# Edge messages of a graph network: more tiles fetched row by row on the SyncE queue, and the receivers of four groups by one DMA

## The chip, the cores and the metric

The kernel runs on one core of one Trainium2 chip. The metric is the device time of one execution in microseconds (us). Before the change it is 4115.59 us, the median of three runs (4114.87 to 4116.8).

## The reference, cut to what matters

One layer of message passing over 12,500 nodes (64 numbers each) and 412,500 edges (32 numbers each), the edges sorted by their receiver. In float32:

```python
h = jnp.maximum(_layernorm(x, axis=-1), 0.0)
msg_in = jnp.concatenate([h[senders], h[receivers], edge_features], axis=-1)
messages = act(msg_in @ W1 + b1) @ W2 + b2          # act is swish
att_logits = act(msg_in @ Wa1 + ba1) @ Wa2 + ba2
att = jax.nn.softmax(att_logits, axis=0)             # over all edges
aggregated = jax.ops.segment_sum(messages * att, receivers, num_segments=N)
upd_in = jnp.concatenate([h, aggregated], axis=-1)
x = x + act(upd_in @ Wu1 + bu1) @ Wu2 + bu2
```

## The kernel before, in words

**Node stage.** The normalized nodes are multiplied once by the sender's and once by the receiver's part of both first-layer weights. The results are two tables in DRAM, `ts_d` (senders) and `tr_d` (receivers), with 128 float32 numbers per node: a row of 512 bytes.

**Edge stage** (`one_pass`). 128 edges make a tile, K = 8 tiles a group, and there are 403 groups. `load(g)` is called two groups ahead of use (AHEAD = 2). For one group it

- issues, on GpSimd (POOL), one indirect DMA for each tile (L487), which fetches the 128 sender rows of the tile into `gs`, a tile with eight buffers;
- for every fourth group (NQ = 4), issues on SyncE (SP) the edge features of four groups, `eo` (L496: partitions 64 to 127, 8192 bytes each), and the receivers' numbers of the same four groups, `db` (L499: two DMAs, for partitions 0 to 31 and 32 to 63; each repeats one row of 8192 bytes of `dst_row` in its 32 partitions), and loads four window positions into registers (L474). `eo` and `db` have two buffers;
- issues on SP two DMAs for a window of receiver rows, `wins` (L506; three buffers);
- calls `rows(q, g)`, which fetches a part of one tile row by row (next paragraph);
- compares `db` with the window's node numbers on VectorE (DVE, L513), which writes the one-hot half of `eo`, and multiplies it on TensorE (PE, L517) with the window: receiver and edge part of eight tiles in the PSUM tile `pe`.

**Rows.** The last tile of some groups is not gathered by POOL. `QUEUES = [(ENG.SP, 11, 0, 12)]` says: on SP, one tile for every 11 groups, starting from group 0, with 12 rows issued in each group. `numbers` (L433) loads the 128 sender numbers of that tile (L438), half a period ahead. In each group, `rows` (L440) loads the next 12 numbers into SP's registers (L460) and issues 12 DMAs of one row, 512 bytes each (L464), into `one_gs` (two buffers). After 11 groups the tile is complete; that group then issues seven gathers in place of eight (L486), and adds the extra tile by an instruction of its own (L525).

**Then** `begin(g)` adds `pe` and `gs` on DVE (L523) and applies tanh on ScalarE (ACT, L526). `end(g)` forms messages and logits on DVE (L536 to L547). `by_node` (L588, L594) and `put` (L618 to L624) sum messages by receiver with a running maximum for the softmax. Between the groups, small parts of the update stage are prepared.

**Order.** Every engine works off its own list in program order; the order on PE, ACT and DVE is that of the calls. On SP the list of a group is: (every fourth group) `eo`, `db`, registers; `wins`, `wins`; register load; the rows. Completion of SP's DMAs is counted in eight counters, which the built program gives out in turn. A DMA first waits until the previous user of its counter, the eighth DMA before it on SP, has landed. The `wins` DMAs also wait for PE to have read that buffer three groups before.

**Update stage.** After the last group, 13 blocks of nodes are finished and written.

The change touches `QUEUES` and the `db` DMAs in `load`.

Of the kernel before, what the change touches and what calls it, by code (L numbers as in the profile page):

```python
# [49 lines left out]
ENG = mybir.EngineType  # L50
# [11 lines left out]
R = 32  # L62
# [4 lines left out]
E2 = H * P  # L67
# [2 lines left out]
NC = 8  # L70
TABLES = 4

QUEUES = [(ENG.SP, 11, 0, 12)]
EPS = 1e-5
NEG = -3.0e38
BIG = 3.0e38
# [288 lines left out]
def one_pass(tc, n_edges, v):  # L365
    nc = tc.nc
# [4 lines left out]
    ts_d, tr_d, bq_d, xb_d, edge, dst_row = (  # L371
        v[k] for k in ("ts_d", "tr_d", "bq_d", "xb_d", "edge", "dst_row"))
# [10 lines left out]
    with ExitStack() as ctx:  # L383
# [30 lines left out]
        with tc.tile_pool(name="work2", bufs=2) as work2, \  # L414
# [25 lines left out]
            def rows(q, g):  # L440
                engine, every, phase, n_rows = QUEUES[q]
                if g == 0:
                    numbers(q, phase + every)
                if g < phase:
                    return
                at = (g - phase) % every
                g = g - at + every
                if at == 0:
                    rows_at.pop((q, g - every), None)
                    if (q, g) in rows_at:  # L450
                        alone[g] = work2.tile([P, C], F32, name=f"one_gs{q}")
                if at == every // 2:
                    numbers(q, g + every)
                if (q, g) not in rows_at:
                    return
                a = at * n_rows
                n = min(n_rows, P - a)
                if n <= 0:
                    return
                load, regs = nc.values_load_multi_w_load_instructions(  # L460
                    rows_at[q, g][0:1, a:a + n], engines=[engine], min_val=0, max_val=NP - 1,
                    skip_runtime_bounds_check_because=WHY)
                for k in range(n):
                    dma[engine].dma_start(alone[g][a + k:a + k + 1, :], ts_d[bass.ds(regs[k], 1), :])  # L464
# [5 lines left out]
                           ap=[[C, NP + WR - SHIFT], [SHIFT * C, 2], [1, C]])  # L470

            def registers(g, engine, at, base=base_sb, top=NP - 1):
                n = min(NQ, NG - g)
                _, regs = nc.values_load_multi_w_load_instructions(  # L474
                    base[0:1, g:g + n], engines=[engine], min_val=0, max_val=top,
                    skip_runtime_bounds_check_because=WHY)
                for i in range(n):
                    at[g + i] = regs[i]

            def load(g):  # L480

                t = g * K
                if g % NQ == 0:
                    registers(g, ENG.SP, at_sp)
                gs = gss[g] = gather.tile([P, K, C], F32, name="gs")
                for j in range(K - (g in alone)):  # L486
                    nc.gpsimd.indirect_dma_start(  # L487
                        out=gs[:, j, :], out_offset=None, in_=ts_d[:, :],
                        in_offset=bass.IndirectOffsetOnAxis(ap=src_sb[:, t + j:t + j + 1], axis=0))
                if g % NQ == 0:  # L490
                    n = min(NQ, NG - g) * E2
                    eo = work2.tile([P, NQ, E2], F32, name="eo")
                    db = work2.tile([WR, NQ, E2], I32, name="db")
                    for i in range(g, min(g + NQ, NG)):
                        ees[i] = eo[:, i - g, :], db[:, i - g, :]
                    nc.sync.dma_start(eo.rearrange("p g e -> p (g e)")[WR:, :n],  # L496
                                      edge[:, g * E2:g * E2 + n])
                    for r in range(2):
                        nc.sync.dma_start(  # L499
                            db.rearrange("p g e -> p (g e)")[r * R:(r + 1) * R, :n],  # L500
                            bass.AP(tensor=dst_row.tensor, offset=dst_row[r:r + 1, g * E2:].offset,
                                    ap=[[0, R], [1, n]]))
                eo, db = ees.pop(g)
                win = wins[g % WINS]
                for r in range(2):
                    nc.sync.dma_start(win[r * R:(r + 1) * R, :, r, :],  # L506
                                      tr_w[bass.ds(at_sp[g], R), :, :])
                for q in range(len(QUEUES)):
                    if QUEUES[q][0] == ENG.SP:
                        rows(q, g)  # L510
                for h in range(2):
                    e = slice(h * E2 // 2, (h + 1) * E2 // 2)
                    pin(nc.vector.tensor_scalar(eo[:WR, e], db[:, e], bj[:, g, h:h + 1], None,  # L513
                                                op0=ALU.is_equal))
                pe = pes[g] = pre_ps.tile([P, K, C], F32, name="pe")
                for q in range(H):
                    pin(nc.tensor.matmul(pe[:, 2 * q:2 * q + 2, :], eo[:, q * P:(q + 1) * P],  # L517
                                         win[:, q // 2, :, :], start=True, stop=True))
# [138 lines left out]
            for g in range(AHEAD):  # L657
                load(g)
            done = 0
            for g in range(NG):  # L660
# [16 lines left out]
                if g + AHEAD < NG:  # L677
                    load(g + AHEAD)
# [358 lines left out]
```

## Time and profile before

| | us |
|---|---|
| median of three runs | 4115.59 |
| the profiled execution | 4115.52 |
| its span, first to last instruction | 4113.8 |
| mean granted TensorE clock | 0.633 |
| first gather starts on POOL | 50.42 |
| first `wins` DMA issued on SP | 86.44 |
| last gather starts on POOL | 4042.24 |
| sum of DVE's waits for `db` at L513 | 151.5 |
| sum of DVE's waits for gathers at L523 | 740.0 |

DMAs by line, of the page's last part: 4608 rows (`one_gs`) of 0.5 KB; 806 windows of 32 KB; 100 `eo` of 512 KB and one of 384; 200 `db` of 256 KB and two of 192; 36 loads of row numbers. The DMA engines are busy 17.0% of the time with SP's queue and 20.8% with POOL's.

A row of a costliest group gives line, engine, operation, what is written and read, how often, the busy time and the mean of one, and then the idle time of the engine before it with what ended it. "Issue" means that the engine waited for nothing the profile shows. SP's and ACT's issuing of DMAs is not counted as busy; it is read from their order of time, where a row names start, duration and, if several equal instructions follow each other, their number. Rows of waits give the total in us, the number of waits and the longest.

### The profile page before, as it was taken

What the parts mean: (1) busy time and instruction counts of PE and PEld (TensorE: products, weight loads), DVE (VectorE), ACT (ScalarE), POOL (GpSimd) and SP (SyncE); (2) the same over time, 40 slices, a digit from 0 to 9 for tenths busy, and PEclk for the clock granted to TensorE, in tenths of its full rate; (3) what the DMA queues carried; (4) which work ended last, traced back from release to release, by engine and by line L of the source; (5) the groups of instructions that cost most, each with busy time, mean ns of one, the idle gap of its engine ahead of it and who ended that gap; (6) DMA issues with size and microseconds to landing.
All of it is one profiled execution on the core that took longest, in us unless ns stands there. A gap on an engine that the chain in (4) does not pass through costs nothing.

```text
span 4113.8 us, 59789 instructions
## 1 busy us (share of the span) xinstructions
PE 2284.8 (56%) x10980; PEld 1852.9 (45%) x10980; DVE 3021.4 (73%) x8518; ACT 584.3 (14%) x1235; POOL 3035.8 (74%) x3213
## 2 busy tenths in 40 slices
PE   5555545555556555556555555555555555555555
PEld 4444434444445444444444444444444444444444
DVE  6777867777777777777777777777777777777777
ACT  3211111111111111111111111111111111111112
POOL 3777777777777777777777777777777777777773
PEclk8666666666565666665566666666666556566665
DMA  7344443443434333333333333333333333333334
GB/s 270 88 102 101 99 105 92 105 101 97 102 93 99 86 91 84 88 91 81 91 84 89 91 81 91 83 89 91 81 91 82 91 91 81 92 81 90 91 78 112
DMA packets 220602, 393.50 MB, mean 96 GB/s; under 512 B 77077, under 2 KB 146554, under 8 KB 207034
## 3 DMA queue, kind: packets, MB, share of 16 engines
q0 software_dynamic: 102016, 209.13, 20.8%
q1 hardware_dynamic: 116826, 170.81, 17.0%
q10 hardware_dynamic: 1376, 9.67, 0.6%
q14 instruction: 294, 2.41, 0.2%
q8 instruction: 90, 1.47, 0.2%
HBM read 363.58 MB, written 25.72 MB: 95 GB/s over the span
## 4 chain that ended last, share of the span: by engine, by line


## 5 line engine op out<-in xcount | busy, mean ns | idle before, releaser
L487 POOL DMA_INDIRECT gs<-ts_d,src_sb x3188 | 3018.7, 947 | 1022.1 <-issue 952.1
L517 PE MATMUL pe<-wins,eo 128*128 128x256 f32 x3224 | 1477.3, 638 | 967.7 <-DVE eo L513 819.6
L517 PEld LDWEIGHTS pe<-wins,eo 128*128 128x128 f32 x3224 | 1000.5, 325 | 1265.8 <-DVE eo L513 970.2
L523 DVE TENSOR_TENSOR gs<-pe,gs 128x1024 f32<-128x1024 f32 (+1 forms) x403 | 487.7, 1211 | 775.5 <-DMA gs<-ts_d,src_sb 740.0
L526 ACT ACTIVATE pe<-gs 128x1024 f32<-128x1024 f32 x403 | 413.8, 1027 | 2585.7 <-DVE gs L523 1997.7
L588 DVE TENSOR_SCALAR wt<-iota_w,dloc,p 128x40 f32<-128x40 f32 x3224 | 734.0, 320 | 0.1
L594 PE MATMUL sp<-wt,acts 128*65 128x40 f32 x6448 | 608.9, 267 | 0.7 <-DVE wt L588 0.7
L594 PEld LDWEIGHTS sp<-wt,acts 128*65 128x65 f32 x6448 | 578.7, 183 | 1.0 <-DVE wt L588 0.8
L605 PEld LDWEIGHTS mt<-ss,w2u 65*128 65x128 f32 x806 | 224.8, 293 | 371.3 <-issue 321.5
L513 DVE TENSOR_SCALAR eo<-db,bj 64x256 f32<-64x256 int32 x806 | 259.7, 360 | 158.6 <-DMA db<-in_dst_row_dram 151.5
L564 PE MATMUL mt<-ident,mx 128*128 128x128 f32 x103 | 45.1, 437 | 547.3 <-DVE sums L622 538.2
L605 PE MATMUL mt<-ss,w2u 65*128 65x40 f32 x806 | 184.9, 324 | 261.4 <-DVE gm L571 257.9
L542 DVE SCALAR_TENSOR_TENSOR pe<-pe,gs 128x512 f32<-128x512 f32 x403 | 281.3, 698 | 13.0
L544 DVE TENSOR_TENSOR pe<-pe,w_all 128x512 f32<-128x512 f32 x403 | 281.4, 698 | 12.8
L536 DVE SCALAR_TENSOR_TENSOR acts<-pe,gs 128x512 f32<-128x512 f32 x403 | 278.2, 690 | 15.7 <-ACT pe L526 4.0
L547 DVE TENSOR_REDUCE lg<-pe 128x8 f32<-128x512 f32 x403 | 278.4, 691 | 13.7
L564 PEld LDWEIGHTS mt<-ident,mx 128*128 128x128 f32 x103 | 18.4, 179 | 557.7 <-issue 556.0
L624 DVE COPY stand<-nmax 64x40 f32 x806 | 163.4, 203 | 0.6
L622 DVE TENSOR_TENSOR sums<-sums,mt 64x40 f32 x600 | 113.2, 189 | 15.0 <-PE mt L605 10.9
L575 ACT ACTIVATE scale<-fall 128x1 f32<-128x1 f32 x103 | 20.9, 203 | 645.1 <-DVE fall L574 629.2
L600 ACT COPY ss<-sp 65x40 f32<-65x40 f32 x403 | 73.5, 182 | 20.7 <-PE sp L594 20.3
L618 DVE SCALAR_TENSOR_TENSOR sums<-sums,scale,mt 64x40 f32 x206 | 51.6, 251 | 11.4 <-PE mt L605 7.3
(92 smaller groups left out, 577.7 us busy)
## 6 DMA issues: line engine op xcount, KB each, us to landing
one_gs<-ts_d SPq DMA_DIRECT2D x4608, 0.5 KB
eo<-in_edge_dram SPq DMA_DIRECT2D x100, 512.0 KB
db<-in_dst_row_dram SPq DMA_DIRECT2D x200, 256.0 KB
gs<-ts_d,src_sb POOLq DMA_INDIRECT x3188
wins<-tr_d SPq DMA_DIRECT2D x806, 32.0 KB
ts_d<-ts SPq DMA_DIRECT2D x5, 896.0 KB
tr_d<-tr ACTq DMA_DIRECT2D x5, 896.0 KB
hT_d<-hT ACTq DMA_DIRECT2D x1, 3136.0 KB
```

What stands on the lines that cost most here:

```text
L487: nc.gpsimd.indirect_dma_start(out=gs[:, j, :], out_offset=None, in_=ts_d[:, :], in_offset=bass.IndirectOffsetOnAxis(ap=src_sb[:, t + j:t ...
L513: pin(nc.vector.tensor_scalar(eo[:WR, e], db[:, e], bj[:, g, h:h + 1], None, op0=ALU.is_equal))
L517: pin(nc.tensor.matmul(pe[:, 2 * q:2 * q + 2, :], eo[:, q * P:(q + 1) * P], win[:, q // 2, :, :], start=True, stop=True))
L523: pin(nc.vector.tensor_tensor(gss[g][:, :n, :], pes[g][:, :n, :], gss[g][:, :n, :], ALU.add))
L526: pin(nc.scalar.activation(pes[g], gss[g], AF.Tanh))
L536: pin(nc.vector.scalar_tensor_tensor(acts[g % ACTS][:, :, 0:U], th[:, :, U:C], 1.0, gs[:, :, U:C], op0=ALU.add, op1=ALU.mult))
L542: pin(nc.vector.scalar_tensor_tensor(att, th[:, :, 0:U], 1.0, gs[:, :, 0:U], op0=ALU.add, op1=ALU.mult))
L544: pin(nc.vector.tensor_tensor(att, att, wa2[:, None, :].to_broadcast([P, K, U]), ALU.mult))
L547: pin(nc.vector.tensor_reduce(lgs[s][:, k:k + K], att, AX.X, ALU.add))
L588: pin(nc.vector.tensor_scalar(wt[:, j, :], iota_w[:, j // H, :], dloc[:, g * K + j:g * K + j + 1], p[:, k + j:k + j + 1], op0=ALU.is_equal ...
L594: pin(nc.tensor.matmul(sp, acts[g % ACTS][:, j, :], wt[:, j, :], start=j == 0, stop=j == K - 1))
L605: pin(nc.tensor.matmul(pp, w2u.rearrange("s h u -> s (h u)"), sps.pop(g), start=True, stop=True))
```

## The change

Two edits:

- `QUEUES` changes from one tile per 11 groups with 12 rows per group to one tile per 9 groups with 16 rows per group. 16 rows in eight groups make 128; in the ninth group none is issued. 44 tiles (5632 rows) are fetched in this way in place of 36 (4608 rows), and POOL issues 3180 gathers in place of 3188.
- The two `db` DMAs for four groups become one. Its source has three dimensions: 2 rows of `dst_row`, each repeated 32 times, 2048 numbers. Its destination is 64 partitions of 2048 numbers.

```diff
@@ -70,7 +70,7 @@
-QUEUES = [(ENG.SP, 11, 0, 12)]
+QUEUES = [(ENG.SP, 9, 0, 16)]
@@ -495,11 +495,10 @@
                     nc.sync.dma_start(eo.rearrange("p g e -> p (g e)")[WR:, :n],
                                       edge[:, g * E2:g * E2 + n])
-                    for r in range(2):
-                        nc.sync.dma_start(
-                            db.rearrange("p g e -> p (g e)")[r * R:(r + 1) * R, :n],
-                            bass.AP(tensor=dst_row.tensor, offset=dst_row[r:r + 1, g * E2:].offset,
-                                    ap=[[0, R], [1, n]]))
+                    a, b = (dst_row[r:r + 1, g * E2:].offset for r in range(2))
+                    nc.sync.dma_start(
+                        db.rearrange("p g e -> p (g e)")[:2 * R, :n],
+                        bass.AP(tensor=dst_row.tensor, offset=a, ap=[[b - a, 2], [0, R], [1, n]]))
```

From there on, the lines of the changed kernel are one lower than those of before: L513 becomes L512, L506 becomes L505, L523 becomes L522.

## The prediction

> **What bounds the kernel now.** I read the busy shares, the slices, the costliest groups, then POOL's order of time, SP's waits and order of time, and the busy time by window. First the page:
>
> ```profile
> PE 2284.8 (56%) x10980; PEld 1852.9 (45%) x10980; DVE 3021.4 (73%) x8518; ACT 584.3 (14%) x1235; POOL 3035.8 (74%) x3213
> ...
> POOL 3777777777777777777777777777777777777773
> ...
> L487 POOL DMA_INDIRECT gs<-ts_d,src_sb x3188 | 3018.7, 947 | 1022.1 <-issue 952.1
> ```
>
> POOL and DVE look equally busy, but POOL's idle time is nearly all "issue": it waits for nobody. Its order of time shows the pitch:
>
> ```profile
> 4012.28 0.94 POOL L487 DMA_INDIRECT gs<-ts_d,src_sb  x1 [0.30 <-issue]
> 4013.53 0.94 POOL L487 DMA_INDIRECT gs<-ts_d,src_sb  x1 [0.30 <-issue]
> ```
>
> The steady pitch is 1.248 us (26 steps take 32.46 us at the end). The gathers run from 50.42 to 4043.18 us; 3188 x 1.248 = 3979 of these 3993 us. So POOL's list of gathers is the bound: 403 groups, 31.6 gathers per four groups, 39.5 us per four groups. DVE needs 3021/403 = 7.5 us per group, 30 us per four.
>
> The second chain is SyncE's. Its waits, and three stretches of its order of time:
>
> ```profile
> SPq L506 <- PE pe L517: 291.7, 69, 9.9
> SPq L506 <- PE mt L605: 256.1, 138, 10.8
> ...
> SPq L464 <- DMA db<-in_dst_row_dram: 88.9, 118, 1.4
> ```
>
> ```profile
> 96.40 0.87 SPq L506 DMA_DIRECT2D wins<-tr_d  x2
> 98.45 4.83 SPq L464 DMA_DIRECT2D one_gs<-ts_d  x12
> 103.53 0.86 SPq L506 DMA_DIRECT2D wins<-tr_d  x2
> ...
> 2038.26 0.49 SPq L496 DMA_DIRECT2D eo<-in_edge_dram  x1
> 2038.80 1.04 SPq L499 DMA_DIRECT2D db<-in_dst_row_dram  x2
> ...
> 2118.98 0.49 SPq L496 DMA_DIRECT2D eo<-in_edge_dram  x1
> 2119.52 1.04 SPq L499 DMA_DIRECT2D db<-in_dst_row_dram  x2
> 2121.36 0.87 SPq L506 DMA_DIRECT2D wins<-tr_d  x2
> 2123.22 6.05 SPq L464 DMA_DIRECT2D one_gs<-ts_d  x12
> ```
>
> A group's undisturbed SP work is 7.10 us (96.40 to 103.53, the next pair 7.10 later), a row (4.83-0.23)/11 = 0.417 us, the head of four groups (eo to wins) 2.38 us. Per four groups that is about 30.1 us, plus about 0.9 us of waiting for db, of 39.5. SP has 8 us to spare, and spends it waiting for PE. The third row of its waits matters most: a row DMA waits for the **receivers' DMA to land**, because SP's DMAs take eight completion counters in turn and each first waits for the eighth one before it. Today that costs at most 1.4 us.
>
> **The change, part by part.**
>
> *Gathers.* 44 tiles in place of 36 leave POOL: 8 x 1.248 = -10.0 us while POOL is the bound. POOL per four groups: 39.4 us. DVE gets 8 more split additions, 8 x (1089+280-1223 ns) = 1.2 us, hidden in its slack.
>
> *Rows.* 8 of 9 groups issue 16 rows, one none. Four rows more are 4 x 0.417 = 1.67 us. The load of row numbers into registers (L460) takes 0.933 us for 12 values and the one at L474 0.488 for 4, so 16 values should take 1.15, +0.22. A group with rows becomes 7.10+1.67+0.22 = 8.99 us; one without about 1.1 us (two wins DMAs at 0.43 and the 0.25 us gap). Four groups on average: 4 x (8 x 8.99 + 1.1)/9 = 32.4. One db issue fewer saves 0.53 of the head: 1.85. The sum is **34.3 us of SP issue per four groups, against POOL's 39.4**. Alone, this would be hidden, with 5.1 us to spare. Eight more loads of row numbers at 0.25 us vanish in it.
>
> *One DMA for the receivers.* Bytes are the same: 64 rows of 8192 B, 524 kB per four groups. What changes is the shape: the source goes from 32 x 2048 (twice) to 2 x 32 x 2048. [...]
>
> What does it cost? The rows on transfers, by window (after PE, PEld, DVE, ACT, POOL: granted clock, DMA share, GB/s):
>
> ```profile
> 1.00:20.00 19.00, 5.97 (x22) 4.51 (x23) 15.30 (x22) 7.91 (x14) 1.14 (x8) 1.00 0.94 362
> 2039.00:2046.00 7.00, 3.19 (x23) 2.71 (x21) 3.29 (x7) 0.00 (x0) 5.17 (x7) 0.74 0.93 202
> 2056.00:2077.00 21.00, 11.94 (x65) 10.12 (x64) 15.59 (x45) 3.13 (x5) 15.83 (x17) 0.66 0.24 61
> ```
>
> Today eo and db of four groups fill all 16 engines for 7 us. A busy engine moves 362/(16 x 0.94) = 24.1 GB/s in the first window and only 202/(16 x 0.93) = 13.6 in the burst; the gathers alone keep each engine 24% busy.
> - Lower end, two engines at 24.1 GB/s and nothing beside: 262 kB / 24.1 = 10.9 us; with the gathers' 24% beside, 14.3 us.
> - Upper end, by the burst: db's half of it, 3.5 us, is 150 GB/s. [...]
> - [...] I take **19.3 us**, between the ends.
>
> Before db's rows come eo's: half of the burst, over at about 2042.4, 3.6 us after the db issue at 2038.80. So db lands L = 3.6+19.3 = 22.9 us after its issue (today: 7).
>
> *Who waits.* In the built program db is followed by two wins DMAs and five rows; the sixth row takes db's counter and waits. SP reaches it 1.31 (to wins) + 1.86 + 0.22 + 5 x 0.417 = 5.5 us after the db issue. The stall is 22.9-5.5 = 17.4 us. Queued behind it on SP are ten rows of this group (4.2 us) and then the wins DMAs of the next group, for which PE's L517 waits, and behind PE DVE's L523. The wins and rows already issued stand behind db in the queue of those engines too, but land right after it. SP runs three groups ahead at most (three wins buffers), so the lead pays for one such stall, not for one every four groups: the mean rate decides. SP per four groups: 34.3+17.4 = **51.7 us, against 39.5 today**. DVE reaches L513 of the new four groups early and waits there for the same landing.
>
> **The sum.** 396 groups issue rows, 99 times four: 99 x (51.7-39.5) = +1208 us. The gathers' -10 us no longer counts, since POOL now waits for gs buffers. At the start SP's first wins (86.4) is 36 us behind POOL's first gather, a lag that today is caught up and then is not; at the end eight groups go without rows, which gives about that back. Own time of the profiled execution 4115.5 (span 4113.8; the median of the runs, 4115.6, is the same): 4115.5+1208 = about **5320 us**.
>
> **The rivals.**
> 1. *SP stalls on the slow db* (above): ends for the transfer 10.9 / 14.3 / 28.0 us give L 14.5 / 17.9 / 31.6, four groups in 43.3 / 46.7 / 60.4, and 4490 / 4830 / 6180 us. Chance 0.80, most of it between 4500 and 5850.
> 2. *db lands in time, not slower*: decided by one point, L below 5.5+5.1 = 10.6 us. That needs the DMA to be spread over well more than two engines (with all 16 it lands after 7 us, as today). Then POOL stays the bound, SP's 34.3 us hide under 39.4, and the time is 4115.5-10.0+1 = about 4106 us, -0.23%. For it: SP's waits of today show 8 us of slack per four groups, and db's own reader, L513, comes 28 us after the issue (2038.80 to 2066.76). [...] Chance 0.13. Its sign is uncertain, since the gain is next to what a measurement can tell from no change (0.2%): 0.06 faster, 0.04 the same, 0.03 slower, if SP's thinner slack costs more than 10 us.
> 3. [...] Chance 0.07.
>
> **Range and chances.** From 4500 (rival 1 at its lower end) to 5850 (a transfer of 24.5 us); outside lie rival 2 and most of rival 3, a fifth. Faster 0.06, same 0.04, slower 0.90.
>
> **What would show it.** Right: SP's L464 waits for db by some 17 us about a hundred times, 1700 us in all, where 88.9 us stand today; DVE's L513 waits for db by many hundreds of us (151.5 today); POOL gets idle time released by something else than issue; the bursts at 0.93 DMA share become long stretches at about 0.3; a group with rows takes 9.0 us on SP between stalls. Wrong: L464's waits for db stay near 1 us and POOL's pitch stays at 1.248 us without gaps (then rival 2); or waits by L506 for PE stay as long as today while the time grows, for then something other than SP's list would be the bound.

## The result, and the profile after

The changed kernel takes 5294.38 us (median of four runs, 5284.78 to 5304.12), the kernel before 4115.23 beside it: ratio 1.2867, 95% interval 1.2852 to 1.2882. The profiled execution has a span of 5287.6 us, 1173.8 more than before. The forecast was 5320.

The page after, with the rows that answer to those of before:

```profile
PE 2227.6 (42%) x10980; PEld 1806.5 (34%) x10980; DVE 2994.4 (57%) x8526; ACT 587.1 (11%) x1235; POOL 3021.3 (57%) x3205
...
POOL 4565645555555655665655565656655556556561
...
L487 POOL DMA_INDIRECT gs<-ts_d,src_sb x3180 | 3004.2, 945 | 2158.1 <-issue 1786.9
...
L512 DVE TENSOR_SCALAR eo<-db,bj 64x256 f32<-64x256 int32 x806 | 265.5, 367 | 2021.3 <-DMA db<-in_dst_row_dram 1981.2
```

But for 3 us on ACT, no engine works longer than before; all wait more. POOL's unbroken row of sevens is gone, and its idle time has doubled. Of its 2158 us before the gathers, 934 are the short steps of about 0.3 us, as before (971). The other 1224 us lie in 119 longer gaps (five before), and these end 0.76 us after DVE has last read a `gs` tile: POOL waits for a `gs` buffer, though the page puts most of this down to "issue".

DVE's comparison, which waited 151.5 us for `db`, waits 1981.2; the row of before was

```profile
L513 DVE TENSOR_SCALAR eo<-db,bj 64x256 f32<-64x256 int32 x806 | 259.7, 360 | 158.6 <-DMA db<-in_dst_row_dram 151.5
```

SP's waits after, and its order of time over one set of four groups:

```profile
SPq L464 <- DMA db<-in_dst_row_dram: 1385.5, 98, 17.5
...
SPq L505 <- PE sp L593: 26.1, 87, 0.4
SPq L505 <- PE mt L604: 21.0, 18, 7.0
```

```profile
2032.53 0.52 SPq L496 DMA_DIRECT2D eo<-in_edge_dram  x1
2033.09 0.57 SPq L499 DMA_DIRECT2D db<-in_dst_row_dram  x1
2034.78 0.89 SPq L505 DMA_DIRECT2D wins<-tr_d  x2
...
2037.56 19.70 SPq L464 DMA_DIRECT2D one_gs<-ts_d  x16
2057.51 0.85 SPq L505 DMA_DIRECT2D wins<-tr_d  x2
2059.77 6.47 SPq L464 DMA_DIRECT2D one_gs<-ts_d  x16
2066.49 0.86 SPq L505 DMA_DIRECT2D wins<-tr_d  x2
2068.74 6.80 SPq L464 DMA_DIRECT2D one_gs<-ts_d  x16
```

Sixteen rows take 6.47 us, but 19.70 right after a `db` DMA: one of them stands still for 13 us. That happens 98 times, 14.1 us on average, where 118 waits of 0.75 us stood before. SP's waits for PE at the windows, 647 us before, have shrunk to 57: SP is now the engine for which the others wait.

The stretches from one `eo` issue to the next, called sets below, show this best. In the 66 sets from the 33rd on, in which no part of the update stage is prepared, a set takes 50.00 us: 34.6 us of SP's own list, 14.85 us of waiting for `db`, 0.55 us of all other waits. Before, it took 39.37: 29.3 us of SP's list, 0.9 of waiting for `db`, 9.2 of other waits, nearly all for PE.

Where the DMA's time goes is seen in windows of the same stretch (the last two columns are the busy share of the 16 DMA engines and GB/s):

```profile
2035.00:2037.00 2.00, 0.00 (x0) 0.00 (x0) 0.00 (x0) 0.00 (x0) 1.65 (x2) 0.50 0.98 218
2037.00:2039.00 2.00, 0.00 (x0) 0.00 (x0) 0.00 (x0) 0.00 (x0) 1.39 (x3) 0.50 0.42 97
...
2047.00:2049.00 2.00, 0.00 (x0) 0.00 (x0) 0.00 (x0) 0.00 (x0) 0.00 (x0) 0.50 0.12 43
2049.00:2051.00 2.00, 0.00 (x0) 0.00 (x0) 0.00 (x0) 0.00 (x0) 0.00 (x0) 0.50 0.13 46
2051.00:2053.00 2.00, 0.00 (x0) 0.00 (x0) 0.42 (x2) 0.00 (x0) 0.00 (x0) 0.50 0.04 13
```

Until 2037 `eo` fills all engines (0.98). From 2047 to 2051 nothing but `db` moves, and the share is 0.12 to 0.13 of 16: **two engines**, 43 to 46 GB/s in all. PE, DVE and ACT do nothing from 2037 to 2051.

### The profile page after: what moved, and what is told of

Same layout as the page of the kernel before. It is cut to its first block, busy times and chain, and to the rows that moved or that the text cites. A ratio compares the mean times of both kernels' runs of the same rounds, so it can differ in the third digit from the quotient of the medians.

```text
span 5287.6 us, 62688 instructions
## 1 busy us (share of the span) xinstructions
PE 2227.6 (42%) x10980; PEld 1806.5 (34%) x10980; DVE 2994.4 (57%) x8526; ACT 587.1 (11%) x1235; POOL 3021.3 (57%) x3205
## 4 chain that ended last, share of the span: by engine, by line
## 5 line engine op out<-in xcount | busy, mean ns | idle before, releaser
L516 PE MATMUL pe<-wins,eo 128*128 128x256 f32 x3224 | 1417.5, 616 | 2500.3 <-DVE eo L512 1444.0
L516 PEld LDWEIGHTS pe<-wins,eo 128*128 128x128 f32 x3224 | 964.3, 313 | 2794.1 <-DVE eo L512 1952.3
L512 DVE TENSOR_SCALAR eo<-db,bj 64x256 f32<-64x256 int32 x806 | 265.5, 367 | 2021.3 <-DMA db<-in_dst_row_dram 1981.2
L587 DVE TENSOR_SCALAR wt<-iota_w,dloc,p 128x40 f32<-128x40 f32 x3224 | 711.3, 307 | 0.1
L522 DVE TENSOR_TENSOR gs<-pe,gs 128x1024 f32<-128x1024 f32 (+1 forms) x403 | 484.8, 1205 | 51.7 <-DMA gs<-ts_d,src_sb 24.3
L563 PEld LDWEIGHTS mt<-ident,mx 128*128 128x128 f32 x103 | 17.4, 169 | 332.9 <-issue 332.3
L322 PE MATMUL mt<-hb,w_all 65*64 65x512 f32 (+1 forms) x50 | 41.5, 928 | 72.6 <-DMA hb<-hT_d 69.4
```

Source lines behind the costliest of these rows:

```text
L522: pin(nc.vector.tensor_tensor(gss[g][:, :n, :], pes[g][:, :n, :], gss[g][:, :n, :], ALU.add))
L587: pin(nc.vector.tensor_scalar(wt[:, j, :], iota_w[:, j // H, :], dloc[:, g * K + j:g * K + j + 1], p[:, k + j:k + j + 1], op0=ALU.is_equal ...
```

## The experiments

The runs used four chips. On three of them the kernel before took 6341 to 6363 us, on the fourth 4114, nearly as in the result. The three are called the 6350-us chips below. Ratios from them can't be set beside 1.287; what is different there is in the last section. "Theory A" below is the prediction's: SP is held by the counter of the late `db`. "Theory B" is that the additional rows overload SP. "Theory C" is that the late landing hurts by itself, since DVE's comparison waits for `db` in order.

The table gives, beside the times, SP's waits for `db` at the rows, and the landing: from the issue of `eo` until the last of the 128 rows of 8192 bytes of `eo` and `db` is through, the median over the sets in the trace's records of DMA packets. In the two kernels without rows the issue runs so far ahead that this isn't comparable.

| kernel | us | before, same chip | ratio (95%) | SP waits for db | landing |
|---|---|---|---|---|---|
| rows alone | 6782.6 | 6353.5 | 1.070 (1.065–1.074) | 37 us | 6.75 us |
| rows alone, again | 6819.6 | 6363.5 | 1.071 (1.067–1.074) | 35 | 6.76 |
| one db DMA alone | 7439.4 | 6353.5 | 1.171 (1.167–1.176) | 1106 | 18.6 |
| one db DMA alone, again | 7439.2 | 6363.5 | 1.169 (1.165–1.173) | 1098 | 18.3 |
| no rows, one db DMA | 5700.4 | 6353.5 | 0.898 (0.895–0.901) | 20 (at the windows) | – |
| no rows, two db DMAs | 5700.6 | 6353.5 | 0.898 (0.894–0.901) | 0 | – |
| both edits, again | 7803.8 | 6341.4 | 1.230 (1.226–1.234) | 1097 | 18.5 |
| both, one DMA of 32 x 2 rows | 6941.2 | 6341.4 | 1.095 (1.093–1.098) | 4 | 6.4 |
| two DMAs of 4 x 8 rows | 4314.3 | 4114.4 | 1.049 (1.047–1.050) | 346 | 10.7 |
| two DMAs of 2 x 16 rows | 4842.6 | 4114.4 | 1.177 (1.175–1.179) | 869 | 16.3 |
| db from POOL's queue | 4980.9 | 4114.4 | 1.210 (1.208–1.213) | 15 (once) | – |
| before | 4115.0 | 4114.4 | – | 73 | – |

**1. The two edits apart.** The rows alone:

```diff
-QUEUES = [(ENG.SP, 11, 0, 12)]
+QUEUES = [(ENG.SP, 9, 0, 16)]
```

> Rows of 9 groups by 16, receivers still by two DMAs. If the single receivers' DMA is the whole loss (SP stalls on its landing): SP issues 34.3+1.4 us per four groups under POOL's 39.4, so about 4106 us, 8 gathers x 1.248 us less than before; L464's waits for db stay near 1 us each, about 100 us in all. If the rows are part of the loss (SP's list too long): above 4300 us, with gaps in POOL's gathers.

The other edit alone is the changed kernel with `QUEUES` as before.

> Rows as before (11 groups by 12), receivers by one DMA. In the changed kernel that DMA lands 19.5 us after its issue. If SP's stall decides: SP per four groups 27.7 + head 2.25 + stall 14.0 = 44.0 us against POOL's 39.5, 99 x 4.5 = +446 us, and with the extra DMAs of the update stage's preparation up to 550: 4560 to 4670 us. If the late landing itself decides, whatever SP does beside it (DVE waits for db at the comparison, in order): 5200 to 5300 us, as with both edits. If the rows were the cause: about 4116 us.

Both ran again on a second of the 6350-us chips, with the same ratios.

> The rows alone again, on another chip if there is one: on the first chip the kernel before took 6354 us in place of 4115, with engines standing still for 15 us and more where nothing is waited for, so its times cannot be set beside the result. If the receivers' DMA is the whole loss: about 4106 us where before takes 4115 (ratio 0.998). If the rows are part of it: above 4300 us (ratio over 1.04).

> The receivers' single DMA alone, rows as before, again. If SP's stall decides: 4560 to 4670 us where before takes 4115 (ratio 1.11 to 1.135), L464 waiting for db about 14 us a hundred times. If the late landing decides whatever SP does: 5200 to 5300 us. If only the rows matter: 4115 us.

The times came out between the theories, because SP has no slack on these chips: in the rows alone, its own list takes 63.9 of the 65.05 us of a set. The waits tell more than the times. With the DMA alone (the second run of it):

```profile
SPq L464 <- DMA db<-in_dst_row_dram: 1098.3, 98, 15.8
```

The kernel is 1076 us slower than before, and SP stands still for 1098 us at this one place: on a chip where SP's list is the bound, a us of stall is a us of time. The rows alone cost 7% there without any such stall, so theory B is true on these chips for that part. What they cost on a chip like the result's wasn't measured.

**2. No rows at all.** `QUEUES = []`, with one and with two `db` DMAs.

> No rows on SP, all tiles gathered by POOL, receivers by one DMA. With no rows the counter of db comes round three groups later, so SP is never held by it. If SP's stall is what hurts: POOL bound, 36 gathers more than before, 4115.5 + 36 x 1.248 = 4160 us, although db lands as late as in the changed kernel (18 to 20 us after issue). If the slow landing hurts by itself, or by crowding the gathers' engines: 4700 us or more, with DVE waiting for db for over 1000 us.

> No rows on SP, receivers by two DMAs as before: the control of the run with one DMA and no rows. All theories: 4160 us, POOL bound. The difference of the two is what the DMA's shape costs where nothing waits for its counter: 0 by the stall theory, over 500 us by the other.

Both take 5700 us; they differ by 0.2 us, which is no difference. Without rows, `db`'s counter comes round three groups later. SP's wait for it at the windows is

```profile
SPq L505 <- DMA db<-in_dst_row_dram: 19.8, 5, 7.0
```

and DVE waits for `db` once, 7.2 us. So the two-engine DMA is harmless by itself when it is issued early. This doesn't separate theory A from C, as it was meant to: without rows SP's own list is 10.4 us of a set of 54.4, SP waits at the windows for most of the rest, and its lead would have hidden a stall as well as a late landing. Section 4 separates them. The 4160 us of the expectation can't be judged on these chips.

**3. The changed kernel there, and one DMA of another shape.**

> The changed kernel itself, beside the kernel before on the same chip, so that the other runs have it as their yardstick. If the chip is like the one of the result: ratio 1.287. If it is like the two chips of the runs so far (before at 6354 to 6363 us): SP's list is the bound there too, the receivers' DMA alone gave 1.170 and the rows alone 1.070, and both together should give 1.22 to 1.28.

The second keeps one DMA and turns its source around. Partitions then alternate between the two rows, and windows and node numbers are laid out to match:

```diff
-    ap=[[b - a, 2], [0, R], [1, n]]
+    ap=[[0, R], [b - a, 2], [1, n]]
...
-    nc.sync.dma_start(win[r * R:(r + 1) * R, :, r, :],
+    nc.sync.dma_start(win[r:2 * R:2, :, r, :],
```

> Both edits kept, but the single receivers' DMA reshaped: source 32 x 2 x 2048 in place of 2 x 32 x 2048, so that partitions alternate between the two rows (the windows and the node numbers are laid out to match). One DMA, same bytes, outermost size 32. If the outermost size sets the number of engines: db lands within 8 us, SP's waits for db fall from 14 us to about 1 us each, and the time is that of the rows alone or a little less: 4106 us where before takes 4115, or about 6780 where before takes 6354. If merging two DMAs into one is what hurts, in whatever shape: as the changed kernel, ratio 1.22 to 1.29.

The same number of bytes in the same number of DMAs: the landing falls from 18.5 to 6.4 us, SP's waits for `db` at the rows from 1097 us to 4, the ratio from 1.230 to 1.095 (the rows' line is L466 in this kernel):

```profile
SPq L466 <- DMA db<-in_dst_row_dram: 3.9, 18, 0.4
```

Merging isn't what hurts; the outermost 2 is. It stays above the rows alone (1.070), probably for a reason of its own: the window DMAs, now to every second partition, take a median of 0.60 us to issue in place of 0.33. Over 806 of them that would be 0.27 x 806 = 218 us on an SP without slack; the two ratios differ by some 160 us. No run isolated it.

**4. The landing time varied**, on a chip like that of the result. Rows of 9 groups by 16 and two DMAs for 32 partitions each, whose source has 4 or 2 as its outermost size:

```diff
-    ap=[[0, R], [1, n]]
+    ap=[[0, 4], [0, R // 4], [1, n]]      # the other kernel: 2 in place of 4
```

> [...] On these chips the changed kernel's last receivers' row lands 18.5 us after the eo issue and SP waits 11.3 us for it each time; with 16 engines it is 6.8 us and SP waits 0.4. If the landing time sets SP's stall: landing at 9.5 to 11.5 us, a stall of 2 to 4 us, and a ratio of 1.10 to 1.13, between the rows alone (1.070) and the changed kernel (1.230). If any narrow DMA is as bad as another: 1.23.

> [...] In the changed kernel many rows take 0.60 us and others 0.31 to 0.35. [...]

SP's waits for `db` in the two kernels, the outermost 4 first:

```profile
SPq L464 <- DMA db<-in_dst_row_dram: 345.9, 176, 4.1
```

```profile
SPq L464 <- DMA db<-in_dst_row_dram: 869.1, 193, 5.9
```

The first landing is as expected. The second is 16.3 us, just outside the author's estimate of 14 to 16, which took rows of about 0.33 us; its ratio, 1.177, lies within that estimate's 1.16 to 1.19. The ratio of the first kernel was expected for a chip where SP has no slack, and is lower here (1.049). Now there are three points on chips of one kind. Over the 66 sets in which no preparation of the update stage runs:

| | landing | a set | SP's list | SP waits for db | other waits of SP |
|---|---|---|---|---|---|
| 4 x 8 rows | 10.70 us | 40.06 us | 35.3 | 4.1 | 0.7 |
| 2 x 16 rows | 16.33 | 45.50 | 35.3 | 9.5 | 0.7 |
| changed kernel | 20.62 | 50.00 | 34.6 | 14.9 | 0.6 |
| before | 7.07 | 39.37 | 29.3 | 0.9 | 9.2 |

5.63 us of landing cost 5.44 us, 4.29 more cost 4.50: **a us later is a us lost, in every such set**. The last three columns decide for theory A. In all three kernels SP either works off its list or waits for `db`'s counter. Were DVE's wait for `db` the bound by itself, SP would run into the full window buffers and wait for PE, as it does before; it no longer does. DVE's own wait follows from the stall, since the next `db` is issued later too. The same holds for another rival. A part of the windows issued after `db` lands only when `db` does. In the set above, 112 packets of 512 bytes start from 2036.36 to 2037.42, none until 2050.92, and 21 from there to 2052.30, which is two sixteenths of the two windows' 128 and the five rows issued before the stall. The first 8 of them follow a row of `db` that ends at 2050.91, the other 13 its last, which ends at 2051.98. PE's waits for the windows grew:

```profile
PE pe L517 <- DMA wins<-tr_d: 66.9, 16, 7.1
...
PE pe L516 <- DMA wins<-tr_d: 579.5, 130, 34.2
```

(before, then the changed kernel). But a late window, too, would let SP run ahead until it waits for PE. Drawn on, the line through the three points meets POOL's 39.4 us at a landing of about 10; that the landing is hidden from there down wasn't measured with 16 rows.

The second kernel shows something else too. Its source has an outermost 2, like that of the changed kernel, and `db` is still through 4.3 us earlier. Of the last 40 rows of `db` in a set, by the packet records, 95% take at most 0.36 us here, and 58% in the changed kernel, where 8% take 0.58 to 0.66 (0.03% here) and the rest lie between or beyond. Beside the number of DMAs, the kernels differ in two things. The two halves of a DMA go to partitions 32 apart in the changed kernel and 16 apart here; and they read two rows of `dst_row` there, and one and the same row here. No run separates the two.

**5. The receivers' DMA on another queue**, in the narrow shape (`nc.gpsimd.dma_start` in place of `nc.sync.dma_start`).

> The changed kernel with its single receivers' DMA, in the same narrow shape, issued from POOL's queue in place of SP's, so that no DMA of SP has its counter; the rows stay on SP. If SP's wait for the counter decides: SP's waits for db vanish and the ratio is that of the rows alone, about 1.07, though db still lands late. If the late landing decides: 1.20 or more, with DVE's comparison waiting for db as in the changed kernel (2190 us). A delay on POOL, whose gathers take turns in counters of their own, is possible; there POOL has over 1000 us of slack.

It didn't isolate what it was to isolate. SP waits for `db` once in all (14.6 us), but the trap moved: POOL's gathers take turns in eight counters of their own. POOL's order of time after a `db` DMA:

```profile
2024.62 0.74 POOL L499 DMA_DIRECT2D db<-in_dst_row_dram  x1
...
2033.20 0.94 POOL L487 DMA_INDIRECT gs<-ts_d,src_sb  x1 [0.30 <-issue]
2040.39 0.94 POOL L487 DMA_INDIRECT gs<-ts_d,src_sb  x1 [6.25 <-DMA gs<-ts_d,src_sb]
```

and over the kernel

```profile
L487 POOL DMA_INDIRECT gs<-ts_d,src_sb x3180 | 3012.9, 947 | 1793.4 <-issue 899.7 <-DMA gs<-ts_d,src_sb 463.3 <-DMA db<-in_dst_row_dram 297.7
```

The gather at 2040.39 is the eighth DMA after `db` on POOL and takes `db`'s counter; the last row of `db` was through at 2039.69. The profile names a gather there, as it does for most of these waits, but 91 waits with 719 us in all are those of the eighth gather after a `db`. The gathers' idle time is 771 us more than before, and issuing 101 `db` DMAs takes another 75; that is 846 of the 862 us by which the profiled span is longer. So the same stall shows on a second queue. DVE's comparison waits 1552 us for `db` here as well, so the time alone doesn't decide between A and C.

**6. The kernel before**, for its profile on a 6350-us chip:

> The kernel before, for a profile on a chip of this kind: about 6350 us. If SP's list is the bound here, SP waits for almost nothing (under 100 us for PE at the windows, 745 us in the profile of the result's chip), and POOL has gaps; the time beyond 4115 us lies in stretches in which SP's instructions follow each other at 0.7 us each and not at 0.06 to 0.28.

It ran on the 4114-us chip (4115.0 us), so the question stays open; the changed kernel's trace of section 3 is used for it below.

## Why the prediction was right, point by point

- *POOL's gathers are the bound before, SP has about 8 us to spare per four groups.* Right for the 66 sets without preparation: 9.2 us of other waits, of which 8.8 are for PE. An average hid the rest. In the 26 sets in which SP also issues the preparation's loads and stores, its list before is 33.3 us, and of 5.4 us of other waits only some 0.3 are for PE; the others are for the DVE, ACT and DMA steps of that work. There SP had little to spare.
- *Two engines.* No run of before shows that the merged DMA has only two; it was the author's assumption. The changed kernel shows it: 0.12 to 0.13 of 16 engines busy while only `db` moves. With an outermost 32 in place of 2 the landing returns from 18.5 to 6.4 us; to merge the two transfers was a loss in this shape.
- *A row of SP's list 0.417 us, a group with rows 8.99.* Measured 8.97 to 8.98 (2059.77 to 2068.74; 2057.51 to 2066.49). The load of 16 numbers has a median of 1.154 us (trace of the rows alone), estimated 1.15.
- *db lands 22.9 us after its issue.* Too long: 20.62 less 0.56 between the two issues is 20.1. **The mis-sized term is the 19.3 us of the transfer.** No run shows it, nor the upper end of 28.0; both rested on assumptions of the author on what two engines move together. What the runs showed in its place: the transfer took about 16.5 us, nearer to the 14.3 that the trace alone had given. A row of 0.60 us goes at 8192/0.60 = 13.6 GB/s, but of a set's last 40 rows just 8% are so long, and 58% take at most 0.36 us, some 23 GB/s and more for each engine. In the kernel with 2 x 16 rows `db` lands 4.3 us earlier, so the long rows of the changed kernel cost that much at most. Rival 3 stood for 28.6 us, an estimate for one engine at 24.1 GB/s with the gathers' 24% beside; it is excluded.
- *A stall of 17.4 us.* 14.1, for the same reason.
- *51.7 us per four groups.* 50.00 in the 66 sets without preparation of the update stage. The head from `eo` to `wins` is 2.25 us, not 1.85.
- *99 x 12.2 = 1208 us.* (The 396 groups include 44 that issue no rows; the 32.4 us per four groups had that in.) In the trace the sets give: 66 without preparation, 3300.3 against 2598.2 us, +702 or 10.6 each; 26 with preparation, 1394.4 against 1026.0, +368 or 14.2 each; four beside these, in which SP catches up before (31.8 us each) and can't after (48.8), +68; the first two, +42; the last two, -12. Together 1169 of the 1174 us. The sum had left the preparation out: in those 26 sets SP's list takes 37.6 us and its other waits 3.7, and with a stall of 12.4 a set takes 53.6 us in place of 50.0. **So the total is closer than its terms, by luck**: a transfer taken too long by 3 us, and work and catching up that weren't counted, cancel.
- *POOL waits for gs buffers, DVE for db, bursts become long.* All seen, at 1981 us for DVE and 1386 for SP (1700 forecast).

The rival "db lands in time" was decided by the point named for it, a landing 10.6 us after the db issue. The kernel with 4 x 8 rows comes to about 9.4 to 10.1 by its records and its sets of groups are at 40.06 us, so the point is about right, or a little lower.

Open: what the rows alone, or the wide single DMA, do on a chip like the result's. The prediction had the rows alone hidden, with 5.1 us to spare per four groups. In the 66 sets of the kernel with 4 x 8 rows SP's list and other waits are 36.0 us without the stall, so there they would be. In its 26 sets with preparation they are 38.5 + 3.6 = 42.1 us, over the 39.46 of before: an estimate of 26 x 2.6 = 70 us lost, more than the 10 us of gathers. No kernel was found that beats the kernel before there. On the 6350-us chips the kernels without rows do, at 0.898 of before.

## What to carry to other kernels

Before merging two DMAs, write down the outermost size of the merged one's source: here a 2 ("two rows, each repeated") left 2 of 16 DMA engines busy (0.12 to 0.13), and turning the dimensions around brought the landing from 18.5 to 6.4 us at the same byte count. A DMA's landing can cost its issuing queue, not only its reader, when a later DMA of that queue needs the same completion counter: here the eighth after `db`, in all 101 sets, and 1386 us of SP's waits. Count how many issues lie between. When a stall repeats at every turn of a loop, as this one did (98 times, 14.1 us each, behind three window buffers), buffers ahead don't hide it: compare the sums per turn, with every DMA of that queue in them. And take the slack of a queue by stage: SP's was 9 us in most sets and little in a quarter of them.

## What the runs showed of the hardware that wasn't expected

**Slow rows in one of two shapes with an outermost 2.** In the changed kernel, where the halves of `db` go to partitions 32 apart, 42% of the last 40 rows of 8192 bytes of a set take more than 0.36 us; with two DMAs of 2 x 16 rows, where the halves of each lie 16 apart, 5%. That goes with 4.3 us of landing and 9% of the time (1.287 against 1.177). Whether the distance of the partitions or the two source rows make it is open.

**An instruction stream that crawls.** On the 6350-us chips, the same kernel's instructions on SP follow each other at times at about 0.70 or 1.40 us each, with no wait shown. Of 6026 steps from the first to the second instruction of a row's or window's issue, the median is 0.073 us in both traces of the changed kernel, the 90th percentile 0.08 on the result's chip and 0.72 here. In the order of time of the rows alone, two groups of the same 16 rows stand close to each other:

```profile
3048.65 32.67 SPq L464 DMA_DIRECT2D one_gs<-ts_d  x16
...
3083.95 6.47 SPq L464 DMA_DIRECT2D one_gs<-ts_d  x16
```

In the changed kernel the steps within the issues of rows and windows take 6.39 ms in place of 3.95, which is 2.43 of the 2.51 ms between the two chips. The cause is open. Late blocks of instructions are a guess that the trace doesn't support: of 154 stretches of at least five slow steps in it, 5% end within 2 us after an 8192-byte packet of the instruction queue, and of random moments 8% lie so. What it means for experiments: there SP's list is the bound in every kernel with rows that was profiled, and an edit's ratio is another one than on the result's chip.
